# First layer of a spectral network: convolution and inverse column transform as one set of 32x32 matmuls

## Chip, cores and metric

The kernel runs on one core of one Trainium2 chip. The metric is the time of one execution on the device in microseconds; lower is better. All data are float32.

## What is computed

The input is a batch of 8 images, 8 channels, 256 x 256 pixels. Two residual steps follow each other. The first adds a small Fourier neural operator on the normalised input; the second adds a 3 x 3 dilation (a running maximum) of the normalised sum.

```python
x = x + fno(group_norm(x))
x = x + dilate3x3(group_norm(x))

def fno(x):                       # 4 groups of 2 channels; grid = row and column coordinate
    h = concat([x, grid])         # 4 inputs per group
    h = gconv1x1(h, fc0)          # 4 groups of 10 channels
    for i in range(4):
        h1 = spectral_conv(h)     # keep 24 x 12 frequencies, mix channels there, go back
        h2 = gconv1x1(h, w[i])
        h = h1 + h2
        if i < 3:
            h = gswish(h)
    return gconv1x1(gswish(gconv1x1(h, fc1)), fc2)   # 10 -> 128 -> 2 per group
```

fc0 is linear, so in the first layer it is folded into what follows: the first convolution h2 is a map from the two channels of x in a group (and constants) to ten channels, and its weights are the product of fc0 and w[0].

## The kernel before, in words

**State.** The state of a whole image stands in the tile `h`, 128 partitions x 11 chunks x 4 x 512. Image rows are spread over blocks, so that 32 partitions (a quarter, called q below) hold 3 blocks of 10 channels and two spare ones. Quarters are groups g in the layers with even number and parts of the rows in the odd ones; f counts the other of the two. One chunk c is 4 x 512 pixels for each partition.

**A layer.** `layers` runs four layers for each image. In each, `spectrum_h` (or `spectrum_x` ahead of layer 0) gets the small spectrum, `mix` multiplies it by the layer's weights and puts the result into the tile `fz`, and `rows_of` does the inverse transform along image rows with matmuls of `fz` against the table `rowg`, which leaves for each image row a vector of at most 32 spectral values in the tile `zt`: 24 of the transform, one constant, one linear term, six zeros. `layer` then goes over the 11 chunks. For each it issues a **burst** (line numbers of the profile in brackets):

- 16 matmuls of the 1x1 convolution, each on one 32x32 square of the array (L452; in layer 0 L449, where the moving operand is six rows of x and the weights are `wcn`)
- 8 matmuls of the inverse column transform, 256 columns each, `zt` as weights of 32 x 128 and the table `binv` as moving operand, added in PSUM (L455)
- two activations by ScalarE that empty the PSUM tiles `p_z` into `h` (L461, in layer 3 L463)

After the burst follow the transposes of the chunk before (`turn`, L424, copied by L194) and the forward transform of the chunk before that (`transform`, L437 and L438), and then steps of other work.

**x for layer 0.** The rows of x that layer 0 reads are loaded into `h` by `read_x` (L469): six partitions of each group and chunk, 4 loads of 48 KB a chunk, on SP's queue. A chunk of `h` is free for them when layer 3 of the image before has stored it in DRAM (L465).

**Other work beside it.** The output head of an image (fc1, fc2) runs beside the layers of the next image: `first` (L588, activation L590) and `second` (L610, added by VectorE at L615) work on slices of the stored state, loaded as `hs` on SP's queue (L580). The dilation of the image before that (`dilate`) runs in between on VectorE, with its loads on POOL's queue. The last head, that of image 7, runs alone.

**Order.** The program writes out the order of TensorE, VectorE and ScalarE by hand, through generators: each yields the number of head steps to be put at that place, for layers 0 to 2 by `CHUNK = (2, 1, 1)`, one entry per chunk in turn. The order on SP and POOL is chosen by the scheduler. PSUM is used as four tiles of two banks, handed out in turn:

```python
def ps_z(name):
    return ps.tile([128, 2, 512], F32, tag="z", bufs=4, name=name)
```

Each engine takes its instructions in order. The first layer of image 0 has no head beside it.

In `mix` for layer 0, L378 makes a constant from the mean, L379 adds it into `fz`, and L383 copies another row of constants; then `copy` (L194) brings the folded spectrum from PSUM into `fz`. The per-image scale (one over the standard deviation) is `mr[:, 1:2]`, and L476 multiplies the weights `wc` by it to give `wcn`.

Of the kernel before, what the change touches and what calls it, by code (L numbers as in the profile page):

```python
# [10 lines left out]
F32 = mybir.dt.float32  # L11
AF = mybir.ActivationFunctionType
ALU = mybir.AluOpType
# [5 lines left out]
HW = 256  # L19
NPIX = HW * HW  # L20
G = 4
WID = 10
# [10 lines left out]
NBLK = 3  # L33
NCH = 11
NQ = 4
# [10 lines left out]
def fno_dilate_kernel(ctx: ExitStack, tc: tile.TileContext, a: dict, out: bass.AP):  # L46
    nc = tc.nc
    mm = nc.tensor.matmul
    PE, DVE, ACT = mybir.EngineType.PE, mybir.EngineType.DVE, mybir.EngineType.Activation

    const = ctx.enter_context(tc.tile_pool(name="const", bufs=1))
    sb = ctx.enter_context(tc.tile_pool(name="sb", bufs=2))
# [10 lines left out]
    def part(i):  # L63
        return slice(32 * i, 32 * i + 32)
# [10 lines left out]
    def load(name, shape, eng=nc.gpsimd):  # L75
        t = const.tile(list(shape), F32, tag=f"c_{name}", name=f"c_{name}")
        eng.dma_start(t, a[name])
        return t

    load_x(0)  # L80
    beta_p = load("beta_p", (128, 4))
    beta_a = const.tile([128, 4 * G], F32, tag="c_beta_a", name="c_beta_a")
# [6 lines left out]
    fc0c = load("fc0c", (128, 3))  # L89
    wbd = load("wbd", (128, WID, G))  # L90
    wt = load("wt", (128, 4, G, 32))
    eh0 = load("eh0", (128, 3, 2, 32), nc.sync)
    xe = load("xe", (128, 6, G, 5), nc.sync)
    wext = const.tile([128, G, WID, 5], F32, tag="c_wext", name="c_wext")
# [3 lines left out]
    rowg = load("rowg", (128, NBLK, NQ, CS))  # L98
    binv = load("binv", (128, HW))
# [5 lines left out]
    edge = load("edge", (128, 4))  # L105

    h = const.tile([128, NCH, NQ, PIX], F32, tag="h", name="h")
    yin = const.tile([128, DR + 2, HW + 2], F32, tag="yin", name="yin")
    nc.vector.memset(yin, -BIG)
    y_rows = [dram.tile([C * HW + 2, HW], F32, tag=f"y{i}", bufs=1, name=f"y_rows{i}") for i in range(2)]  # L110
# [3 lines left out]
    zt = const.tile([128, CS, NQ, 32], F32, tag="zt", name="zt")  # L114
# [3 lines left out]

    def softplus(t, n, name):
        e = const.tile([128, n], F32, tag=f"{name}_e", name=f"{name}_e")
        nc.vector.tensor_scalar(e, t, -1.0, None, ALU.mult)
        nc.vector.tensor_tensor(e, e, t, ALU.max)
        nc.scalar.activation(e, e, AF.Exp, scale=-1.0)
        nc.vector.tensor_scalar(e, e, 1.0, None, ALU.add)
        nc.scalar.activation(e, e, AF.Ln)
        sp = const.tile([128, n], F32, tag=f"{name}_sp", name=f"{name}_sp")
        nc.vector.tensor_scalar(sp, t, 0.0, None, ALU.max)
        nc.vector.tensor_tensor(sp, sp, e, ALU.add)  # L130
        nc.vector.tensor_scalar(sp, sp, 1e-20, None, ALU.max)
        rs = const.tile([128, n], F32, tag=f"{name}_rs", name=f"{name}_rs")
        nc.vector.tensor_scalar(rs, sp, 1.1, None, ALU.mult)
        nc.vector.reciprocal(rs, rs)
        return sp, rs

    sp_p, rs_p = softplus(beta_p, 4, "bp")
    sp_a, rs_a = softplus(beta_a, 4 * G, "ba")  # L140
    io = const.tile([128, 4 * G], F32, tag="io", name="io")
    nc.vector.tensor_copy(io[:, 0:4], sp_a[:, 0:4])
    nc.vector.tensor_tensor(io[:, 4:12], sp_a[:, 4:12], rs_a[:, 0:8], ALU.mult)
# [3 lines left out]
        nc.vector.tensor_scalar(w2[:, g, :], w2[:, g, :], rs_a[:, 12 + g : 13 + g], None, ALU.mult)  # L147


    wc = const.tile([128, 32], F32, tag="wc", name="wc")  # L150
    p = ps_z("p_wc")
    for g in range(G):
        mm(p[32 * g : 32 * g + 6, 0, :32], fc0x[part(g), :], wt[part(g), 0, g, :], start=True, stop=True)
# [7 lines left out]
    nc.vector.memset(wm, 0.0)  # L161
    for g in range(G):
        nc.vector.tensor_scalar(wm[32 * g : 32 * g + 2, :, g], wc[32 * g : 32 * g + 2, :WID], -1.0, None, ALU.mult)
    cv = const.tile([3, WID, G], F32, tag="cv", name="cv")
    nc.vector.tensor_tensor(
        cv, p[:3, 1, : WID * G].rearrange("p (o g) -> p o g", o=WID),
        sp_a[:3, 0:4].unsqueeze(1).to_broadcast([3, WID, G]), ALU.mult,
# [177 lines left out]
    def mix(b, l, out_):  # L345

        s = [sb.tile([128, 3, G, 2, WID], F32, tag=f"S{i}", bufs=1, name=f"S{i}_{b}_{l}") for i in range(2)]
        bt, sw = out_["bt"], out_["sw"]
        for k in range(3):
            for k2 in range(2):  # L350
                pr = turned[:, 2, 1024 * k2 : 1024 * k2 + 800].rearrange("p (g m i) -> p g m i", g=G, i=WID)
                nc.vector.tensor_tensor(  # L352
                    pr, sw[k], bt[:, k2, k].unsqueeze(2).to_broadcast([128, G, 2 * WID, WID]), ALU.mult)
                yield 0.7
                nc.vector.tensor_reduce(  # L355
                    s[k2][:, k].rearrange("p g s o -> p (g s o)"),
                    pr.rearrange("p g m i -> p (g m) i"), AX.X, ALU.add,
                )
                if k == 0 and k2 == 1:
                    sw.append(load_sw(l, 2))  # L360
                yield 0.7
        f = sb.tile([128, 2, 3, G, WID], F32, tag="F", bufs=1, name=f"F_{b}_{l}")
        nc.vector.tensor_tensor(f[:, 0], s[0][:, :, :, 0, :], s[1][:, :, :, 1, :], ALU.subtract)
        nc.vector.tensor_tensor(f[:, 1], s[0][:, :, :, 1, :], s[1][:, :, :, 0, :], ALU.add)
        yield 0.5

        p = ps_a(f"p_f_{b}_{l}")
        for slot in range(2):
            for n, (table, part_of) in enumerate(((0, slot), (1 + slot, 1 - slot))):
                for q in range(4):  # L370
                    mm(p[part(q), 120 * slot : 120 * slot + 120], fold[part(q), table, :],
                       f[part(q), part_of].rearrange("p k g o -> p (k g o)"), start=n == 0, stop=n == 1)
        nc.vector.tensor_copy(fz[0:32, :, :, 24], cz[:, l])
        if l == 0:
            mr = out_["mr"]
            d = sb.tile([128, 1], F32, tag="d", name=f"dm_{b}")
            nc.vector.tensor_tensor(d, mr[:, 0:1], mr[:, 1:2], ALU.mult)
            mm(p[0:1, 240 : 240 + WID * G], d, wm.rearrange("p o g -> p (o g)"), start=True, stop=True)  # L378
            nc.vector.tensor_tensor(  # L379
                fz[0:1, :, :, 24], fz[0:1, :, :, 24],  # L380
                p[0:1, 240 : 240 + WID * G].rearrange("p (o g) -> p o g", o=WID), ALU.add)
        if l < 2:
            nc.vector.tensor_copy(fz[0:32, :, :, 25], cz[:, 4 if l == 0 else 3])  # L383
        for q in range(4):
            dst = fz[part(q), :, :, 6 * q : 6 * q + 6].rearrange("p o g k -> p k g o")
            src = p[part(q), :240].rearrange("p (k g o) -> p k g o", g=G, o=WID)
            copy(q, dst, src)
        yield 2.5
# [27 lines left out]
    def layer(b, l, out_, stored, side):  # L416
        group_in_f = l % 2 == 1
# [23 lines left out]

        def burst(c):
            pair = [ps_z(f"p_z_{b}_{l}_{c}_{i}") for i in range(2)]
            for f in range(NQ):
                for q in range(NQ):
                    o = pair[q // 2][part(f), q % 2, :]
                    if l == 0:
                        k = slice(32 * q, 32 * q + 6)
                        mm(o, wcn[k, :], h[k, c, f, :], start=True, stop=False)  # L449
                    else:  # L450
                        g = f if group_in_f else q
                        mm(o, wt[part(q), l, g, :], h[part(q), c, f, :], start=True, stop=False)  # L452
            for s in range(2):
                for q in range(NQ):
                    mm(pair[q // 2][:, q % 2, HW * s : HW * (s + 1)],  # L455
                       zt[part(q), 2 * c + s].rearrange("p f o -> p (f o)"), binv[part(q), :],
                       start=False, stop=s == 1)
            for i in range(2):
                dst = h[:, c, 2 * i : 2 * i + 2, :]
                if l < 3:  # L460
                    nc.scalar.activation(dst, pair[i], AF.Silu)  # L461
                else:
                    nc.scalar.activation(dst, pair[i], AF.Identity, bias=bias3)  # L463
            if l == 3:
                nc.sync.dma_start(stored[c], h[:, c].rearrange("p f w -> p (f w)"))  # L465

        def read_x(c):
            for g in range(G):
                nc.sync.dma_start(  # L469
                    h[32 * g : 32 * g + 6, c].rearrange("p f w -> p (f w)"), a["xp"][b, c, g])  # L470

        if l == 0:
            for c in range(NCH):
                read_x(c)
            wcn = sb.tile([128, 32], F32, tag="wcn", bufs=1, name=f"wcn_{b}")
            nc.vector.tensor_scalar(wcn, wc, out_["mr"][:, 1:2], None, ALU.mult)  # L476
        room = 0.0
        yield ()
        for c in range(NCH):
# [36 lines left out]
        yield from then  # L516


    spare = h.rearrange("p c f w -> p (c f w)")
    ya = spare[:, : 18 * (HW + 2)].rearrange("p (r w) -> p r w", r=18)  # L520
    ma = spare[:, 6144 : 6144 + 18 * HW].rearrange("p (r w) -> p r w", r=18)
    oa = spare[:, 12288 : 12288 + 16 * HW].rearrange("p (r w) -> p r w", r=16)
# [225 lines left out]
def _tables():  # L748
# [4 lines left out]
    real = row_of >= 0  # L753
# [20 lines left out]
    rowg[:, : NM + 1] = np.where(real, np.cos(ang), 0.0)  # L774
    rowg[:, NM + 1 : 2 * NM + 1] = np.where(real, np.sin(ang), 0.0)[1:]
    rowg[0, 2 * NM + 1] = np.where(real, line[row_of], 0.0)
    fold = np.zeros((4, 32, 3, 32))
    for i in range(2 * NM):
        m, sign = (i, 1.0) if i < NM else (2 * NM - i, -1.0)
# [9 lines left out]
    binv[:, at + 3] = -c * np.sin(_angle(np.outer(ky, w)))  # L789
    binv[:, 2 * NM] = 1.0  # L790
    binv[:, 2 * NM + 1] = line


    planes = [np.broadcast_to(line[:, None], (HW, HW)), np.broadcast_to(line, (HW, HW)), np.ones((HW, HW))]
    xe = np.zeros((4, 32, 2, 3, G, 5))
    for j, v in enumerate(planes):
# [12 lines left out]
        "rowg": rowg.reshape(128, NBLK, NQ, CS),  # L809
        "fold": fold.reshape(128, 3, 32), "binv": binv.reshape(128, HW),  # L810
        "xe": xe.reshape(128, 6, G, 5), "grp": grp, "edge": edge,
    }
    return {k: np.ascontiguousarray(v, f32) for k, v in tables.items()}

# [65 lines left out]
```

## Time and profile before

| | us |
|---|---|
| median of 3 runs | 4306.66 |
| lowest and highest run | 4306.16, 4310.51 |
| the profiled execution, its own time | 4309.43 |
| span of its instructions | 4307.7 |
| TensorE busy | 4089.1 |
| ScalarE busy | 2772.9 |
| VectorE busy | 2297.3 |
| layer-0 convolution matmuls (L449), busy | 115.0 |

The profile is of one execution. PE is TensorE's matmuls, PEld its weight loads, DVE VectorE, ACT ScalarE, SP the engine that issues most DMAs. A group of instructions is one row: line, engine, operation, output and inputs by the program's names, shapes, count, then the busy time in us and the mean duration in ns of one instruction, then the idle time of the engine just before them and what ended it. Each float32 matmul of the program appears as two instructions in the profile,[...] so the 1408 matmuls of L449 count 2816. Busy times of matmuls overlap, as up to 16 run together; what a group costs is seen from its start to the start of the next. In a timeline, the columns are the start and the length in us, the engine, the line, the operation and how many instructions were merged. In a row for a stretch, the columns are its ends, its length, the busy time (and number of instructions) of PE, PEld, DVE, ACT and POOL, then the granted clock of TensorE, the busy share of the DMA engines and GB/s.

### The profile page before, as it was taken

The page shows a single profiled execution, that of the slowest core. Times are in us where ns is not written, and L with a number is a line of the kernel's source. Part 1 is how long each engine was busy: PE and PEld are TensorE (multiplying, and loading weights), DVE is VectorE, ACT ScalarE, POOL GpSimd, SP SyncE. Part 2 cuts the span into 40 slices and gives each one's busy share as a digit, 9 for nine tenths or more (in the row PEclk, how much of TensorE's full clock was granted, in tenths as well). Part 3 has the DMA queues.
Part 4 walks back from the last instruction along what each step waited for, and adds up shares of the span by engine and source line. Part 5 has one row for each costly group of instructions (what it writes and reads, how often), then busy time and mean ns, then how long its engine had stood idle before and what let it go on. Part 6 is the DMA issues. An engine that isn't in the chain of part 4 may idle for free. (4 is left out here: it accounts for less than half of the span.)

```text
span 4307.7 us, 115455 instructions
## 1 busy us (share of the span) xinstructions
PE 4089.1 (95%) x52330; PEld 1925.6 (45%) x52330; DVE 2297.3 (53%) x3424; ACT 2772.9 (64%) x2886; POOL 117.0 (3%) x202
## 2 busy tenths in 40 slices
PE   5877999999999999999999999999999999999997
PEld 3544454444443444434444354444454444444222
DVE  4444544555655555655556555655655555654433
ACT  3435656766667666576666756667666766567887
POOL 1000000000000000000000000000000000000000
PEclk8988999999999999999999999999999999999999
DMA  2014101332114221242112511134111332114321
GB/s 78 13 40 151 53 28 43 135 103 62 55 53 161 87 62 52 75 171 58 52 59 81 182 42 53 50 104 159 55 45 53 136 120 62 48 57 147 109 60 46
DMA packets 113682, 344.65 MB, mean 80 GB/s; under 512 B 15611, under 2 KB 18107, under 8 KB 97768
## 3 DMA queue, kind: packets, MB, share of 16 engines
q1 hardware_dynamic: 95000, 276.18, 20.3%
q0 software_dynamic: 18192, 61.08, 4.3%
q8 instruction: 411, 6.73, 0.7%
q14 instruction: 79, 0.65, 0.1%
HBM read 213.21 MB, written 123.74 MB: 78 GB/s over the span
## 5 line engine op out<-in xcount | busy, mean ns | idle before, releaser
L590 ACT ACTIVATE act<-p_fc 128x1024 f32<-128x1024 f32 x2048 | 1968.9, 1025 | 1202.4 <-PE p_fc L588 1200.6
L588 PE MATMUL p_fc<-hs,c_w 32*128 32x512 f32 x8192 | 1191.6, 633 | 15.3 <-DVE turned L194 8.6
L610 PE MATMUL p_fc<-act,c_w 128*32 128x512 f32 x8192 | 986.7, 597 | 38.9 <-ACT act L590 25.6
L194 DVE COPY turned<-p_t 128x1024 f32<-128x1024 f32 x495 | 584.6, 1219 | 707.7 <-PE p_t L424 707.0
L588 PEld LDWEIGHTS p_fc<-hs,c_w 32*128 32x128 f32 x8192 | 383.6, 183 | 622.8 <-issue 240.9
L461 ACT ACTIVATE h<-p_z 128x1024 f32<-128x1024 f32 x528 | 512.9, 1023 | 117.4 <-PE p_z L455 116.7
L424 PE MATMUL p_t<-ident,h 128*128 128x128 f32 x4224 | 525.8, 278 | 0.0
L615 DVE TENSOR_TENSOR y<-p_fc,y 128x512 f32<-128x512 f32 x392 | 270.7, 690 | 474.9 <-PE p_fc L610 473.0
L610 PEld LDWEIGHTS p_fc<-act,c_w 128*32 128x32 f32 x8192 | 229.9, 109 | 647.4 <-issue 333.0
L424 PEld LDWEIGHTS p_t<-ident,h 128*128 128x128 f32 x4224 | 463.3, 142 | 98.5 <-ACT act L590 64.7
L455 PE MATMUL p_z<-c_binv,zt 32*128 32x256 f32 x5632 | 408.6, 404 | 1.0 <-ACT zt L192 1.0
L455 PEld LDWEIGHTS p_z<-c_binv,zt 32*128 32x128 f32 x5632 | 258.3, 185 | 304.4 <-issue 292.7
L452 PE MATMUL p_z<-h,c_wt 32*32 32x512 f32 x8448 | 317.0, 601 | 0.0
L437 PE MATMUL p_d<-turned,c_fw 128*32 128x240 f32 x4224 | 268.1, 371 | 4.1 <-ACT act L590 2.1
L194 DVE COPY zt<-p_g 128x264 f32<-128x264 f32 x300 | 159.0, 626 | 139.8 <-PE p_g L397 75.0
L463 ACT ACTIVATE h<-p_z,c_bias 128x1024 f32<-128x1024 f32 x176 | 186.6, 1111 | 26.4 <-PE p_z L455 25.9
L355 DVE TENSOR_REDUCE S<-turned 128x80 f32<-128x800 f32 x192 | 188.8, 983 | 5.0
L352 DVE TENSOR_TENSOR turned<-t,B 128x800 f32<-128x800 f32 x192 | 188.4, 981 | 0.5 <-DMA t<-in_spw 0.4
L452 PEld LDWEIGHTS p_z<-h,c_wt 32*32 32x32 f32 x8448 | 72.3, 103 | 190.1 <-ACT act L590 85.7
L437 PEld LDWEIGHTS p_d<-turned,c_fw 128*32 128x32 f32 x4224 | 109.6, 108 | 100.4 <-issue 39.1
L194 DVE COPY turned<-p_at 88x1024 f32<-88x1024 f32 x90 | 101.7, 1155 | 73.8 <-PE p_at L313 73.8
L438 DVE COPY zt<-p_d 128x240 f32<-128x240 f32 x264 | 105.5, 400 | 51.1 <-PE p_d L437 51.1
(170 smaller groups left out, 2023.8 us busy)
## 6 DMA issues: line engine op xcount, KB each, us to landing
stored<-h SPq DMA_DIRECT2D x88, 1024.0 KB
hs<-stored SPq DMA_DIRECT2D x352, 256.0 KB
t<-in_spw SPq DMA_DIRECT2D x96, 400.0 KB
yin<-y_rows POOLq DMA_DIRECT2D x56, 512.0 KB, 4.7
h<-in_xp SPq DMA_DIRECT2D x352, 48.0 KB
turned<-in_x SPq DMA_DIRECT2D x16, 1024.0 KB
y<-in_x SPq DMA_DIRECT2D x56, 256.0 KB
y_rows<-y POOLq DMA_DIRECT2D x56, 256.0 KB, 2.4
```

Of the source, the lines that this page charges most:

```text
L194: nc.vector.tensor_copy(dst, src)
L352: nc.vector.tensor_tensor(pr, sw[k], bt[:, k2, k].unsqueeze(2).to_broadcast([128, G, 2 * WID, WID]), ALU.mult)
L355: nc.vector.tensor_reduce(s[k2][:, k].rearrange("p g s o -> p (g s o)"), pr.rearrange("p g m i -> p (g m) i"), AX.X, ALU.add,)
L424: nc.tensor.transpose(t[:, i // 4, 128 * (i % 4) : 128 * (i % 4 + 1)], h[:, c, i // 2, 256 * (i % 2) + 128 * v : 256 * (i % 2) + 128 * (v ...
L437: mm(p[part(g), :240], fw[:, v, :], m[:, :, :, : NBLK * WID], start=v == 0, stop=v == 1)
L452: mm(o, wt[part(q), l, g, :], h[part(q), c, f, :], start=True, stop=False)
L455: mm(pair[q // 2][:, q % 2, HW * s : HW * (s + 1)], zt[part(q), 2 * c + s].rearrange("p f o -> p (f o)"), binv[part(q), :], start=False, s ...
L461: nc.scalar.activation(dst, pair[i], AF.Silu)
L588: mm(pair[g // 2][:, g % 2, :], w1[part(g), blk, :], hs[k][part(g), :], start=True, stop=True)
L590: nc.scalar.activation(act[:, 2 * i : 2 * i + 2, :], pair[i], AF.Silu)
L610: mm(acc[part(g), :], w2[:, g, 15 - rb - i : 47 - rb - i], act[:, g, :], start=i == 0, stop=i == 1)
L615: nc.vector.tensor_tensor(y, sums, y, ALU.add)
```

## The change

In layer 0 the two sets of matmuls of a burst become one. The six spare spectral values are used to carry the convolution: `mix` puts the convolution's weights, scaled by the image's `mr`, into columns 26 to 31 of `fz`, and the table `rowg` gets ones at these places, so that `rows_of` brings them into rows 26 to 31 of each 32 x 32 piece of `zt`. The moving operand has the matching rows in `h`: rows 0 to 25 of each group hold the first 26 rows of `binv`, repeated for each image row (the new table `wave`), and rows 26 to 31 hold the six rows of x. A matmul of a 32 x 32 piece of `zt` with 32 rows of `h` then gives the inverse transform and the convolution together. Each image row has its own piece, so a matmul covers 256 columns, and a burst has 32 of them.

`read_x` loads both parts for each chunk and image: 8 loads a chunk, four of 208 KB from `wave` and four of 48 KB from x. The product `wcn` of each image is replaced by `wsel`. Some small tiles of the setup are moved into the memory of `h` (chunk 10), which the first loads overwrite later.

```diff
+    xrow = load("xrow", (128, 38))
...
+    spare = h.rearrange("p c f w -> p (c f w)")
...
-    sp_p, rs_p = softplus(beta_p, 4, "bp")
-    sp_a, rs_a = softplus(beta_a, 4 * G, "ba")
+    sp_p, rs_p = softplus(beta_p, 4, 22300)
+    sp_a, rs_a = softplus(beta_a, 4 * G, 22320)
...
-    wc = const.tile([128, 32], F32, tag="wc", name="wc")
+    wc = spare[:, 22400:22432]
...
+    ws = spare[:, 22472:22482]
+    nc.vector.tensor_tensor(ws, wc[:, 0:WID], wc[:, WID : 2 * WID], ALU.add)
+    nc.vector.tensor_tensor(ws, ws, wc[:, 2 * WID : 3 * WID], ALU.add)
+    wk = const.tile([128, WID, 6], F32, tag="wk", name="wk")
+    nc.vector.tensor_tensor(
+        wk, ws.unsqueeze(2).to_broadcast([128, WID, 6]),
+        xrow[:, 0:6].unsqueeze(1).to_broadcast([128, WID, 6]), ALU.mult)
...
             nc.vector.tensor_tensor(
                 fz[0:1, :, :, 24], fz[0:1, :, :, 24],
                 p[0:1, 240 : 240 + WID * G].rearrange("p (o g) -> p o g", o=WID), ALU.add)
+
+            wsel = sb.tile([128, 32], F32, tag="wsel", bufs=1, name=f"wsel_{b}")
+            nc.vector.tensor_scalar(wsel, xrow[:, 6:38], mr[:, 1:2], None, ALU.mult)
+            pair = [ps_z(f"p_wk_{b}_{i}") for i in range(2)]
+            for g in range(G):
+                mm(pair[g // 2][0:32, g % 2, : 6 * WID], wsel[part(g), :],
+                   wk[part(g)].rearrange("p o i -> p (o i)"), start=True, stop=True)
+            for i in range(2):
+                nc.vector.tensor_copy(
+                    fz[0:32, :, 2 * i : 2 * i + 2, 26:32].rearrange("p o g i -> p g o i"),
+                    pair[i][0:32, :, : 6 * WID].rearrange("p g (o i) -> p g o i", o=WID))
...
-            for f in range(NQ):
-                for q in range(NQ):
-                    o = pair[q // 2][part(f), q % 2, :]
-                    if l == 0:
-                        k = slice(32 * q, 32 * q + 6)
-                        mm(o, wcn[k, :], h[k, c, f, :], start=True, stop=False)
...
+            if l == 0:
+
+                for s in range(2):
+                    cols = slice(HW * s, HW * (s + 1))
+                    for f in range(NQ):
+                        for q in range(NQ):
+                            mm(pair[q // 2][part(f), q % 2, cols], zt[part(q), 2 * c + s, f, :],
+                               h[part(q), c, f, cols], start=True, stop=True)
...
                 nc.sync.dma_start(
-                    h[32 * g : 32 * g + 6, c].rearrange("p f w -> p (f w)"), a["xp"][b, c, g])
+                    h[32 * g : 32 * g + 26, c].rearrange("p f w -> p (f w)"), a["wave"])
+                nc.sync.dma_start(
+                    h[32 * g + 26 : 32 * g + 32, c].rearrange("p f w -> p (f w)"), a["xp"][b, c, g])
...
-            wcn = sb.tile([128, 32], F32, tag="wcn", bufs=1, name=f"wcn_{b}")
-            nc.vector.tensor_scalar(wcn, wc, out_["mr"][:, 1:2], None, ALU.mult)
...
+    for blk in range(NBLK):
+        rowg[0, 26 + blk, blk] = real[blk]
...
+    xrow = np.zeros((4, 32, 38))
+    for i in range(6):
+        xrow[:, i, i] = 1.0
+        xrow[:, i, 6 + 26 + i // 2] = 1.0
...
+        "xrow": xrow.reshape(128, 38), "wave": np.tile(binv[0, :26], (1, 2 * NQ)),
```

More of the change, by code (lines that the diff above doesn't have):

```diff
@@ L117, in fno_dilate_kernel, with softplus @@
     nc.vector.memset(fz, 0.0)
-    def softplus(t, n, name):
-        e = const.tile([128, n], F32, tag=f"{name}_e", name=f"{name}_e")
+    def softplus(t, n, at):
+        e = spare[:, at + 0 * n : at + 1 * n]
         nc.vector.tensor_scalar(e, t, -1.0, None, ALU.mult)
@@ L127, in softplus @@
         nc.scalar.activation(e, e, AF.Ln)
-        sp = const.tile([128, n], F32, tag=f"{name}_sp", name=f"{name}_sp")
+        sp = spare[:, at + 1 * n : at + 2 * n]
         nc.vector.tensor_scalar(sp, t, 0.0, None, ALU.max)
@@ L131, in softplus @@
         nc.vector.tensor_scalar(sp, sp, 1e-20, None, ALU.max)
-        rs = const.tile([128, n], F32, tag=f"{name}_rs", name=f"{name}_rs")
+        rs = spare[:, at + 2 * n : at + 3 * n]
         nc.vector.tensor_scalar(rs, sp, 1.1, None, ALU.mult)
@@ L163, in fno_dilate_kernel @@
         nc.vector.tensor_scalar(wm[32 * g : 32 * g + 2, :, g], wc[32 * g : 32 * g + 2, :WID], -1.0, None, ALU.mult)
-    cv = const.tile([3, WID, G], F32, tag="cv", name="cv")
+    cv = spare[:3, 22432:22472].rearrange("p (o g) -> p o g", o=WID)
+    ws = spare[:, 22472:22482]
[5 more added lines that the diff above has]
+        xrow[:, 0:6].unsqueeze(1).to_broadcast([128, WID, 6]), ALU.mult)
     nc.vector.tensor_tensor(
@@ L443, in burst @@
             pair = [ps_z(f"p_z_{b}_{l}_{c}_{i}") for i in range(2)]
-            for f in range(NQ):
-                for q in range(NQ):
-                    o = pair[q // 2][part(f), q % 2, :]
-                    if l == 0:
-                        k = slice(32 * q, 32 * q + 6)
[L449 to L457, printed above, removed]
+            if l == 0:
[5 more added lines that the diff above has]
+                               h[part(q), c, f, cols], start=True, stop=True)
+            else:
+                for f in range(NQ):
+                    for q in range(NQ):
+                        mm(pair[q // 2][part(f), q % 2, :], wt[part(q), l, f if group_in_f else q, :],
+                           h[part(q), c, f, :], start=True, stop=False)
+                for s in range(2):
+                    for q in range(NQ):
+                        mm(pair[q // 2][:, q % 2, HW * s : HW * (s + 1)],
+                           zt[part(q), 2 * c + s].rearrange("p f o -> p (f o)"), binv[part(q), :],
+                           start=False, stop=s == 1)
             for i in range(2):
@@ L516, in layers @@
         yield from then
-    spare = h.rearrange("p c f w -> p (c f w)")
     ya = spare[:, : 18 * (HW + 2)].rearrange("p (r w) -> p r w", r=18)
```

## The prediction

> **What bounds the kernel now.** I read the busy shares first, then the chain of waits, then the groups by line, then stretches of the timeline.
>
> ```profile
> PE 4089.1 (95%) x52330; PEld 1925.6 (45%) x52330; DVE 2297.3 (53%) x3424; ACT 2772.9 (64%) x2886; POOL 117.0 (3%) x202
> L455 PE MATMUL p_z<-c_binv,zt 32*128 32x256 f32 x5632 | 408.6, 404 | 1.0 <-ACT zt L192 1.0
> L452 PE MATMUL p_z<-h,c_wt 32*32 32x512 f32 x8448 | 317.0, 601 | 0.0
> L449 PE MATMUL p_z<-h,wcn 6*32 6x512 f32 x2816 | 115.0, 600 | 2.4 <-issue 1.4 <-ACT zt L192 0.8 <-DVE turned L194 0.2
> ```
>
> TensorE is busy 95% of the span, and an idle time of 2.4 us in front of all 88 bursts of L449 says that it does not wait there. The page's chain of waits covers only the last stretch, the head of image 7 running alone, so it says nothing of layer 0; the stretches do. In a table of the eight layer-0 stretches, this is the one of image 2:
>
> ```profile
> 916.00:1003.00 87.00, 85.90 (x1096) 43.64 (x1068) 43.70 (x61) 54.45 (x57) 2.07 (x4) 0.98 0.10 30
> ```
>
> PE 85.9 of 87 us, VectorE 43.7, ScalarE 54.5. A busy TensorE need not be doing useful work, so I took costs from start to start, in one chunk of that stretch (timeline, ScalarE's lines with it):
>
> ```profile
> 947.51 1.14 PE L588 MATMUL p_fc<-hs,c_w 32*128 32x512 f32 x8
> 948.59 1.18 PE L449 MATMUL p_z<-h,wcn 6*32 6x512 f32 x32
> 948.75 1.94 ACT L590 ACTIVATE act<-p_fc 128x1024 f32<-128x1024 f32 x2 [0.99 <-PE p_fc L588]
> 949.70 1.15 PE L455 MATMUL p_z<-c_binv,zt 32*128 32x256 f32 x16
> 950.77 1.97 PE L424 MATMUL p_t<-ident,h 128*128 128x128 f32 x16
> 950.88 1.94 ACT L461 ACTIVATE h<-p_z 128x1024 f32<-128x1024 f32 x2 [0.19 <-PE p_z L455]
> 952.67 1.02 PE L437 MATMUL p_d<-turned,c_fw 128*32 128x240 f32 x16
> 953.62 1.14 PE L588 MATMUL p_fc<-hs,c_w 32*128 32x512 f32 x8
> ```
>
> Each group begins as the one before ends: the burst takes 948.59 to 950.77, that is 1.11 us for the convolution and 1.07 for the inverse transform, 2.18 together. The unit that counts in layer 0 is TensorE time per burst.
>
> [...] the 32 instructions of one L449 group (each matmul is two passes) last 600 ns each, and start to start the group takes 1.11 us. [...]
>
> ```profile
> 48.91 21.94 SPq L469 DMA_DIRECT2D h<-in_xp  x36
> 378.92 21.98 SPq L469 DMA_DIRECT2D h<-in_xp  x30
> ```
>
> give 0.61 and 0.73 us per issue.
>
> **The change, part by part.** *The burst.* Out go 16 matmuls of 512 columns over 16 squares and 8 of 256 columns over four row strips. In come 32 of 256 columns, two for each square, so four passes of 256 columns through a square where L449 has two of 512: the same 1024 columns. Two rows bound the price from below: L449 itself (1.11) and L455, four passes of 256 on four strips (1.07). From above: a matmul lasts 600 ns at 512 columns and 404 at 256, so about 0.21 us is fixed; if the array empties between the halves, 1.11 + 0.21 = 1.32. No group of before sends four passes through all 16 squares, so I take the middle, 1.2. A burst then saves 2.18 - 1.2 = 0.98 us, and 8 images x 11 chunks = 88 bursts save 86 us.
>
> *What becomes late.* The burst was cover for ScalarE. In the chunk above, both PSUM tiles of the head step at 947.51 are emptied by ScalarE from 948.75 to 950.69, 0.97 us each. The transposes that follow the burst reuse them: now at 950.77, after both; then at 949.79, when the first is just free, and its half of L424 (0.95) lasts until the second is. The next steps meet the burst's own tiles (emptied by ScalarE, which goes straight on, at 951.66 and 952.63) at 951.69 and 952.64. So nothing stalls yet, but no margin is left. I charge 0.1 us for each of the 77 chunks with a head beside them: +8 (0 to 0.5 each).
>
> *In mix, once an image.* wcn becomes wsel (0.21 us on VectorE either way), but it stands behind the addition L379, which waits for L378, and the eight new matmul instructions wait for wsel. TensorE, in order, stands for two VectorE operations (about 0.5 us with the signals), then runs 60 columns twice (about 0.4, from L371's 285 ns each): 0.9 x 8 = +7. Behind it wait the next head steps. The two copies into fz (nearest row: 583 ns for 240 elements, so 0.4 each) delay the fz copies; for images 2 to 7 two head steps stand between and hide it (the fz copies end at 900.57, their reader L397 starts at 901.84, and it moves back too), for images 0 and 1 it is exposed: +2.
>
> *Setup.* One more load on POOL's queue (0.56 us of issue ahead of cz, fold and others) and three small VectorE operations: +1. The scratch tiles moved into h are free long before chunk 10 is loaded.
>
> *The loads.* 352 transfers become 704, all on SP, with 73 MB more (352 x 208 KB), against 276 MB on that queue now. [...] the hardware queue's row (276.18 MB in 20.3% of 16 engines' span) makes 0.41 us of 8 KB on average[...] I take 5. What must not be late:
>
> - Image 0: 36 of its 44 loads go out only from 48.91 on. Chunk 10 then lands near 49 + 2 + 50 = 101, and is read at 70 + 10 x 3.9 = 109. Hidden at 5[...].
> - Later images: loads follow the stores of layer 3 (one every 8.2 us, 863.43 to 896.28). Store, head load and the new loads make 3.3 + 0.5 + 5 = 8.8 per chunk on the engines; the excess of 0.6 x 11 = 7 us falls on what stands behind in SP's order, the head's loads of hs and the y loads. A load of hs issued at 882.32 is used at 908.79, 26 us later. Hidden.
> - Image 1: layer 3 of image 0 runs without a head, so 30 loads stood in a row until 400.9, and hs loads behind them; now 20 to 25 us later. I charge 4 in all for images 0 and 1.
>
> Sum: -86 + 8 + 7 + 2 + 1 + 4 = -64 us on the profiled execution, 4309.4 (span 4307.7), so 4245; the median of the runs lies 2.8 below that execution, so **4242 us**.
>
> **The rivals.** *The loads become the bound (slower).* [...] It beats the gain from roughly 7.4 us a chunk. [...] *The squares queue for weights (slower).* If the second half's weights load one square after another, 16 x 0.103 us (L449's load) make a burst of 2.75: 88 x 1.55 more, 4380. L455 and L402 reload in every pass without it, though on four places only. *The time turns into waits for PSUM.* If ScalarE's emptying sets the chunk, only the 11 chunks of image 0 keep the gain: 11 gained less 14 of the other costs, 4310. ScalarE's 54 of 87 us speaks against it. *Part of the gain is lost to late loads in images 0 and 1*, 20 to 40 us: about 4270. That the burst does not shrink at all would need the 16 squares to fail, which L449 excludes.
>
> **How the numbers follow.** Forecast 0.61 (alone 4215 to 4268: burst 1.1 to 1.32, tile waits 0 to 0.3); late loads in part 0.13; PSUM waits 0.05; loads as the bound 0.15; queued weights 0.06. About 0.2% (9 us) is what a measurement here can tell from no change. Faster is the first two less a little, 0.73; the same 0.05; slower 0.22. The range runs from the forecast's lower end to a load pace just past the crossing: 4213 to 4340; beyond it lies most of the two slow cases.
>
> **What would show it.** One group in place of L449 and L455 in layer 0, with 1.1 to 1.3 us from its start to that of L424; 88 bursts, 5632 instructions of 256 columns. Image 0's chunk period 3.9 instead of 4.9 us; layer-0 stretches near 77 instead of 87. SP's issues of L469 at about 0.6 us. Wrong if TensorE shows idle time ended by the loads of h or of hs, if the group takes over 1.4 us, or if L424 waits for ScalarE by more than 0.3 us a chunk.

## The result, and the profile after

The changed kernel takes **4378.35 us** (median of 4 runs, 4375.64 to 4388.06) against 4307.84 (4306.16 to 4310.51) for the kernel before: a ratio of 1.0167, 95% interval 1.015 to 1.0185. The forecast was 4242 and faster; the kernel is 70 us slower. The profiled execution took 4375.64 us, its span 4373.7, that is 66.0 more than the span before.

Line numbers have moved. L471 is the new burst (before L449 and L455), L445 the transposes after it (L424), L458 the transform (L437), L480 and L476 the inverse transform and the convolution of layers 1 to 3 (L455, L452). L612 and L634 are the head's two layers (L588, L610), L637 its first addition into y (L613), L604 and L627 the loads of hs and y (L580, L603), L490 the store (L465), L494 and L496 the loads of wave rows and of x.

From the page of the kernel after, the busy shares, the groups of instructions and the loads:

```profile
PE 4044.6 (92%) x53802; PEld 1925.0 (44%) x53802; DVE 2302.0 (53%) x3443; ACT 2766.3 (63%) x2886; POOL 117.7 (3%) x203
...
L480 PE MATMUL p_z<-c_binv,zt 32*128 32x256 f32 x4224 | 303.4, 400 | 0.6 <-ACT zt L202 0.6
L471 PE MATMUL p_z<-h,zt 32*32 32x256 f32 x5632 | 145.1, 403 | 10.4 <-ACT act L614 7.2
L637 DVE SCALAR_TENSOR_TENSOR y<-p_fc,c_b,y 128x512 f32<-128x512 f32 x56 | 42.1, 751 | 217.2 <-DMA y<-in_x 159.0
...
h<-in_wave SPq DMA_DIRECT2D x352, 208.0 KB
h<-in_xp SPq DMA_DIRECT2D x352, 48.0 KB
```

The change is there: 5632 matmuls in layer 0 in place of 2816 + 1408, and the inverse transform is left to layers 1 to 3. TensorE's busy time fell by 45 us while the span rose by 66, so idle time has come in. The row that names its cause is none of the changed lines: L637, VectorE's addition of the head's sums to y, stood idle for 217.2 us, 159.0 of them until a load of y landed. The stretch of image 2's layer 0, the one shown of before:

```profile
916.00:1003.00 87.00, 73.50 (x1148) 40.35 (x1144) 39.65 (x54) 47.48 (x51) 1.30 (x2) 0.86 0.28 77
```

TensorE is busy for 73.5 of 87 us instead of 85.9, at a granted clock of 0.86 instead of 0.98, with a DMA share of 0.28 instead of 0.10. The waits (in total, times, longest) of the kernel after, from TensorE's, VectorE's and SP's tables:

```profile
PE p_fc L612 <- DVE mr_y L214: 55.0, 4, 17.5
...
PE p_fc L612 <- DVE y L637: 29.5, 2, 16.6
...
DVE y L637 <- DMA y<-in_x: 159.0, 6, 29.2
...
SPq L494 <- DMA h<-in_wave: 127.7, 176, 4.2
```

Six waits of VectorE for y, and six stops of TensorE behind VectorE (the first two rows, 55.0 + 29.5 = 84.5 us together): one for each of images 2 to 7. There was no such row before. In the last row SP itself waits, in the row of new loads, until earlier loads of the row have landed.

**One stop from its cause to its end**, in image 2. SP's timeline, the last store of layer 3 and then the last of the new loads with what stood behind them:

```profile
889.59 0.35 SPq L490 DMA_DIRECT2D stored<-h  x1
...
928.79 0.31 SPq L494 DMA_DIRECT2D h<-in_wave  x1
929.18 0.27 SPq L496 DMA_DIRECT2D h<-in_xp  x1
930.29 0.35 SPq L604 DMA_DIRECT2D hs<-stored  x1
930.74 0.38 SPq L627 DMA_DIRECT2D y<-in_x  x1
```

Of the image's 88 loads, 47 are issued after that store, and they fill 40 us (with other loads between them); before, 5 of 44 were. Only when the last is out does SP come to y, at 930.74. In the kernel before:

```profile
912.26 0.33 SPq L603 DMA_DIRECT2D y<-in_x  x1
```

So y is issued 18.5 us later, though TensorE had reached the step earlier than before, and VectorE can go on 5.4 us after that, at 936.15. VectorE's timeline of the kernel after:

```profile
936.15 0.75 DVE L637 SCALAR_TENSOR_TENSOR y<-p_fc,c_b,y 128x512 f32<-128x512 f32 x1 [24.47 <-DMA y<-in_x]
936.82 0.15 DVE L214 COPY mr_y<-p_st_y 128x1 f32<-128x1 f32 x1
937.33 2.35 DVE L204 COPY turned<-p_t 128x1024 f32<-128x1024 f32 x2
```

VectorE takes these instructions in the written order: it stands before the addition for 24.47 us, and behind it wait the statistics (L214, at 936.82) and the copies out of the transposes (L204, at 937.33), which TensorE needs. TensorE's timeline:

```profile
922.39 3.68 PE L445 MATMUL p_t<-ident,h 128*128 128x128 f32 x16 [1.05 <-ACT h L486]
936.96 2.14 PE L612 MATMUL p_fc<-hs,c_w 32*128 32x512 f32 x8 [10.89 <-DVE mr_y L214]
...
939.74 2.83 PE L471 MATMUL p_z<-h,zt 32*32 32x256 f32 x64
...
1481.47 1.14 PE L612 MATMUL p_fc<-hs,c_w 32*128 32x512 f32 x8
1482.54 1.50 PE L471 MATMUL p_z<-h,zt 32*32 32x256 f32 x64
1483.96 1.97 PE L445 MATMUL p_t<-ident,h 128*128 128x128 f32 x16
```

TensorE issues what it can and stands for 10.89 us. The last three lines are an undisturbed chunk: there the burst takes 1.42 us from its start to that of L445, and L612 and L471 last half as long as just after the stop.

**The ledger.** I took TensorE's time from the start of each group to the start of the next (the group's slot), summed by line, and compared the two executions. The burst gives 57.7 back (its own waits in it). The transposes, in whose slots the stops fall, take 89 more; the head's first layer 9.6, mix 8, the statistics 8, the transform 5 and the spectral rows 3. The sum is +65, of the 66 in the spans.

### The profile page after: what moved, and what is told of

The parts are those of the page before. It is cut to its first block, busy times and chain, and to the rows that moved or that the text cites. A ratio compares the mean times of both kernels' runs of the same rounds, so it can differ in the third digit from the quotient of the medians.

```text
span 4373.7 us, 118951 instructions
## 1 busy us (share of the span) xinstructions
PE 4044.6 (92%) x53802; PEld 1925.0 (44%) x53802; DVE 2302.0 (53%) x3443; ACT 2766.3 (63%) x2886; POOL 117.7 (3%) x203
## 5 line engine op out<-in xcount | busy, mean ns | idle before, releaser
L612 PE MATMUL p_fc<-hs,c_w 32*128 32x512 f32 x8192 | 1203.0, 637 | 105.8 <-DVE mr_y L214 55.0
L634 PE MATMUL p_fc<-act,c_w 128*32 128x512 f32 x8192 | 987.4, 597 | 38.0 <-ACT act L614 25.5
L204 DVE COPY turned<-p_t 128x1024 f32<-128x1024 f32 x495 | 584.7, 1220 | 637.9 <-PE p_t L445 637.2
L612 PEld LDWEIGHTS p_fc<-hs,c_w 32*128 32x128 f32 x8192 | 387.1, 184 | 718.1 <-issue 226.7
L445 PE MATMUL p_t<-ident,h 128*128 128x128 f32 x4224 | 530.4, 280 | 6.8 <-ACT h L486 6.4
L445 PEld LDWEIGHTS p_t<-ident,h 128*128 128x128 f32 x4224 | 467.1, 143 | 113.8 <-ACT act L614 70.6
L634 PEld LDWEIGHTS p_fc<-act,c_w 128*32 128x32 f32 x8192 | 230.5, 109 | 646.0 <-issue 338.2
L476 PE MATMUL p_z<-h,c_wt 32*32 32x512 f32 x8448 | 318.0, 601 | 0.3 <-issue 0.3
L480 PE MATMUL p_z<-c_binv,zt 32*128 32x256 f32 x4224 | 303.4, 400 | 0.6 <-ACT zt L202 0.6
L480 PEld LDWEIGHTS p_z<-c_binv,zt 32*128 32x128 f32 x4224 | 192.7, 184 | 227.7 <-issue 220.5
L458 PE MATMUL p_d<-turned,c_fw 128*32 128x240 f32 x4224 | 268.1, 371 | 3.1 <-ACT act L614 2.1
L204 DVE COPY zt<-p_g 128x264 f32<-128x264 f32 x300 | 160.3, 624 | 140.0 <-PE p_g L418 74.2
L476 PEld LDWEIGHTS p_z<-h,c_wt 32*32 32x32 f32 x8448 | 72.3, 103 | 191.3 <-ACT act L614 87.2
L637 DVE SCALAR_TENSOR_TENSOR y<-p_fc,c_b,y 128x512 f32<-128x512 f32 x56 | 42.1, 751 | 217.2 <-DMA y<-in_x 159.0
L471 PE MATMUL p_z<-h,zt 32*32 32x256 f32 x5632 | 145.1, 403 | 10.4 <-ACT act L614 7.2
L458 PEld LDWEIGHTS p_d<-turned,c_fw 128*32 128x32 f32 x4224 | 109.7, 108 | 99.4 <-issue 38.7
```

What stands on the lines that cost most here:

```text
L204: nc.vector.tensor_copy(dst, src)
L445: nc.tensor.transpose(t[:, i // 4, 128 * (i % 4) : 128 * (i % 4 + 1)], h[:, c, i // 2, 256 * (i % 2) + 128 * v : 256 * (i % 2) + 128 * (v ...
L458: mm(p[part(g), :240], fw[:, v, :], m[:, :, :, : NBLK * WID], start=v == 0, stop=v == 1)
L476: mm(pair[q // 2][part(f), q % 2, :], wt[part(q), l, f if group_in_f else q, :], h[part(q), c, f, :], start=True, stop=False)
L480: mm(pair[q // 2][:, q % 2, HW * s : HW * (s + 1)], zt[part(q), 2 * c + s].rearrange("p f o -> p (f o)"), binv[part(q), :], start=False, s ...
L612: mm(pair[g // 2][:, g % 2, :], w1[part(g), blk, :], hs[k][part(g), :], start=True, stop=True)
```

## The experiments

The theory, called Q in the expectations: what costs is the order of SP's queue, in which the load of y stands behind the wave rows' loads. The rival, called B: the 73 MB and the transfers themselves cost, wherever they stand. Each ratio is against the kernel before, run on the same chip.

**Move only the load of y to POOL's queue (y_on_pool).** Edit of the kernel after:

```diff
                 box["y"] = y
-                nc.sync.dma_start(
+                nc.gpsimd.dma_start(
                     y, a["x"][b].rearrange(...)[:, t])
```

> The changed kernel with the y loads issued on POOL's queue in place of SP's. Theory Q (the y load of a new head stands behind the loads of wave and x in SP's order, VectorE waits for it, the transposes' copies and with them TensorE wait for VectorE): the 159 us that VectorE waits for y go below 30, the 15 to 20 us stops of TensorE in chunk 1 of images 2 to 7 go, about 4275 to 4300. Rival B (73 MB more traffic slows all transfers): y is late on the other queue too, 4360 to 4380. Rival P (the loss lies on TensorE's own work): no change, 4370 to 4380.

4272.42 us (4271.48 to 4273.27), ratio 0.992 (0.9904 to 0.9937). One word takes 106 us off the changed kernel, with all 704 loads still on SP, and makes it faster than before. That is a little better than Q's 4275. VectorE's wait for y is gone. B can't explain that, for not a byte less is moved, and P can't either, for TensorE's own work is the same. In the stretch of image 2's layer 0 the DMA engines are busier than in the changed kernel (0.39 against 0.28), and TensorE loses nothing:

```profile
916.00:1003.00 87.00, 85.71 (x1352) 44.45 (x1356) 48.57 (x69) 58.52 (x62) 4.99 (x8) 1.00 0.39 104
```

At most the 24 us by which this run lies above the run without these loads (no_wave_loads, below) are left for B. A part of them is a late load of hs in image 1:

```profile
435.99 2.09 PE L612 MATMUL p_fc<-hs,c_w 32*128 32x512 f32 x8 [6.93 <-DMA hs<-stored]
```

The rest of the 24 us was not followed.

**The wave rows' loads alone, in the kernel before (wave_loads_alone).** The rows are loaded and read by no one:

```diff
+                nc.sync.dma_start(
+                    h[32 * g + 6 : 32 * g + 32, c].rearrange("p f w -> p (f w)"), a["wave"])
                 nc.sync.dma_start(
                     h[32 * g : 32 * g + 6, c].rearrange("p f w -> p (f w)"), a["xp"][b, c, g])
```

> The kernel before with the 352 loads of wave added, into 26 rows of h that its layer 0 does not read; its matmuls are untouched. Q: the same order on SP and the same late y load, so slower than before by what the stops cost, 80 to 110 us: 4390 to 4415. B: the same, 4380 to 4415. P: the loads cost nothing, 4308.

4414.59 us (4410.28 to 4418.14), ratio 1.0251 (1.0236 to 1.0266). VectorE's waits:

```profile
DVE y L615 <- DMA y<-in_x: 146.9, 6, 25.9
```

The same six waits come up with the old burst. The loss belongs to the loads, not to the matmuls: 108 us of it without any of the rest of the change. This rules out P; Q and B expected nearly the same here.

**The change without these loads (no_wave_loads).** Only image 0 gets them:

```diff
-                nc.sync.dma_start(
-                    h[32 * g : 32 * g + 26, c]..., a["wave"])
+                if b == 0:
+                    nc.sync.dma_start(
+                        h[32 * g : 32 * g + 26, c]..., a["wave"])
```

> The changed kernel with the loads of wave left out for images 1 to 7 (those images' layer 0 then multiplies what layer 3 left in these rows). Q and B: the price of the loads goes and the burst's saving stays (88 x 0.75 = 66, less 8 in mix): 4255 to 4275. P: 4370 to 4380.

4247.93 us (4247.05 to 4253.02), ratio 0.9867 (0.9852 to 0.9881), a little under what was expected. This is the price of everything in the change but 308 loads: 58 us less than before. The loads of images 1 to 7 cost 4378 - 4248 = 130 us. The stretch:

```profile
916.00:1003.00 87.00, 85.88 (x1310) 45.89 (x1314) 51.59 (x70) 56.11 (x59) 3.13 (x5) 1.00 0.15 44
```

In this stretch TensorE is as busy as before the change, at full clock.

**One load for a chunk instead of eight, still on SP (one_load).** The host's table holds wave rows and x together, so 1 MB goes in one transfer:

```diff
-            for g in range(G):
-                nc.sync.dma_start(h[32 * g : 32 * g + 26, c]..., a["wave"])
-                nc.sync.dma_start(h[32 * g + 26 : 32 * g + 32, c]..., a["xp"][b, c, g])
+            nc.sync.dma_start(h[:, c].rearrange("p f w -> p (f w)"), a["xw"][b, c])
```

> The changed kernel with one load of 1 MB per chunk, wave and x laid out together in DRAM by the host, in place of eight: the same bytes into the same rows, 88 transfers in place of 704. Q: SP is free 30 us earlier, y is not late: 4250 to 4275, faster than both. B: the bytes are the same, so 4350 to 4380. P: 4370 to 4380.

4338.06 us (4335.71 to 4342.22), ratio 1.0075 (1.006 to 1.009). My number was missed: y is now on time, but another load is late. VectorE's wait and SP's wait:

```profile
DVE turned L362 <- DMA t<-in_spw: 82.9, 8, 29.9
...
SPq L493 <- DMA stored<-h: 589.7, 74, 10.1
```

and SP's wait in the kernel before:

```profile
SPq L469 <- DMA stored<-h: 292.8, 67, 6.2
```

SP's timeline with the single load:

```profile
907.86 0.33 SPq L493 DMA_DIRECT2D h<-in_xw  x1
908.28 0.45 SPq L352 DMA_DIRECT2D t<-in_spw  x1
...
917.36 0.33 SPq L493 DMA_DIRECT2D h<-in_xw  x1
917.78 0.38 SPq L352 DMA_DIRECT2D t<-in_spw  x1
...
927.22 0.33 SPq L493 DMA_DIRECT2D h<-in_xw  x1
```

In the program a chunk's load comes after the store that empties its rows. SP stands at that wait until the store has landed, 74 times, for 589.7 us, and each of mix's loads of spectral weights (L352) leaves only after it, 9 to 10 us apart. It is the same fault with another victim: a load that waits, ahead of one that is needed. Whether SP's waits or the bytes are the cause is what the next run asks.

**The same single load on POOL's queue (one_load_on_pool).**

```diff
-            nc.sync.dma_start(h[:, c]..., a["xw"][b, c])
+            nc.gpsimd.dma_start(h[:, c]..., a["xw"][b, c])
```

> The one-load kernel with its loads of 1 MB issued on POOL's queue in place of SP's. Its run showed TensorE stopped where mix waits for its third weight load (83 us of VectorE), which stands behind an x load that waits for a store to land. Theory Q (whatever stands behind the x loads in SP's order is late, not the bytes): SP never waits for a store any more, weights, hs and y are on time, 4245 to 4265. Rival B (bytes): 4325 to 4345 as before. A third outcome: y_rows and yin on POOL become the late ones, 4290 to 4340.

4260.46 us (4257.33 to 4261.85), ratio 0.9891 (0.9874 to 0.9907): faster than both kernels, by 48 us than before and by 118 than the change as it stood. It moves the same bytes. SP's timeline and the stretch:

```profile
911.83 0.33 SPq L623 DMA_DIRECT2D y<-in_x  x1
```

```profile
916.00:1003.00 87.00, 85.87 (x1333) 44.66 (x1302) 48.65 (x67) 58.54 (x62) 3.13 (x5) 1.00 0.16 46
```

y goes out at 911.83, about when it did before (912.26), and the stretch is that of no_wave_loads. This kernel is 12 us slower than that one. In image 1, mix (L381) waits 20.3 us where it waits 9.3 there, but TensorE comes to it earlier, so the two profiled executions are only 4.3 us apart; the 12 us were not followed further.

**All eight loads a chunk on POOL (eight_loads_on_pool)** asks whether the queue alone is enough. In the kernel after, both lines of the load become `nc.gpsimd.dma_start`.

> The changed kernel with all eight loads a chunk on POOL's queue in place of SP's. Q (only the order on SP mattered): near the one-load kernel on POOL, 4260 to 4275. Rival C (their count costs on any queue, POOL's own y_rows and yin then stand behind them): 4290 to 4350.

4308.73 us (4305.36 to 4312.48), ratio 1.0005 (0.9996 to 1.0014): no change against before. Q's number was missed; the count costs too. The stretch, in which the last of the five engines is POOL:

```profile
916.00:1003.00 87.00, 83.81 (x1212) 43.57 (x1204) 43.85 (x63) 54.24 (x58) 16.39 (x31) 0.96 0.34 84
```

POOL spends 16.39 us here where a single load a chunk needed 3.13, and the DMA share is 0.34 instead of 0.16. Against one_load_on_pool 48 us are lost, in the head's first layer (18), the burst (11), the inverse transform and mix of image 1. I did not find one place or one mechanism for it: it stays open how much is POOL's issue and how much the small transfers.

**Relief of SP alone, in the kernel before (x_on_pool_before)**: its 352 loads of x become `nc.gpsimd.dma_start`. This asks whether POOL's version is faster only because SP had been too full all along.

> The kernel before with its 352 loads of x on POOL's queue and nothing else. Q: before loses nothing to the order on SP (y is on time by 8 us), so 4300 to 4312, and what the changed kernel gains with its loads on POOL is the burst's. Rival (a relieved SP speeds up any version): under 4290.

4312.16 us (4308.16 to 4317.22), ratio 1.0014 (1.0007 to 1.0021). Nothing is gained, so the 48 us of one_load_on_pool are put down to the burst. The test is not quite clean: it issues 352 small loads on POOL, and as eight_loads_on_pool, with 704, is 48 us above one_load_on_pool, with 88, a small gain from a relieved SP could be hidden.

**Why the burst takes 1.42 us and not 1.2.** In the trace of the undisturbed chunk, the first half's squares start about 7 ns apart, and their second passes follow from 240 ns on. The 33rd matmul instruction, by its place the first of the second half, starts at 456 ns, 216 ns after the second pass before it, so without a stop. The 34th starts only at 649 ns, 193 ns later, and the others follow 17 ns apart instead of 7. Three other orders, each in the kernel y_on_pool with nothing else changed:

```diff
# order_s_q_f
-                    for f in range(NQ):
-                        for q in range(NQ):
+                    for q in range(NQ):
+                        for f in range(NQ):
# order_pairs
-                for s in range(2):
-                    for f in range(NQ):
+                for p, s in ((0, 0), (0, 1), (1, 0), (1, 1)):
+                    for f in (2 * p, 2 * p + 1):
# order_f_s_q
-                for s in range(2):
-                    for f in range(NQ):
+                for f, s in ((f, s) for f in range(NQ) for s in range(2)):
+                    for _ in range(1):
```

> The same with order s, q, f: the four squares of one row strip follow each other. W: the first half's start is slower, the group 1.4 to 1.8. D: 1.43 as before.

> The same with the strips in pairs, s inside: 8 squares, their second halves, then the other 8. W: a square comes again after 8; 1.1 to 1.3 if the pairs overlap, about 1.7 to 2.0 if not. D: 1.9 to 2.1.

> The kernel with y on POOL, burst order strip f outermost, then half s, then q: a square's second half follows after 4 matmuls. The group takes 1.43 us with s outermost. Theory W (the second half's weights are admitted in program order, so that a square that comes again late, after the whole first half, waits): coming again after 4 gives no stop between halves but four strips in a row; 1.1 to 1.2 if the strips overlap, 2 to 3.5 if only four squares run at a time. Rival D (all 16 squares must drain before any second half begins): the strips drain four times, over 2.5.

One run each: 4267.76, 4290.95 and 4324.31 us. TensorE's timeline of the three, the burst and what follows it:

```profile
1452.88 1.49 PE L471 MATMUL p_z<-h,zt 32*32 32x256 f32 x64
1454.30 0.88 PE L445 MATMUL p_t<-ident,h 128*128 128x128 f32 x6
```

```profile
1466.53 1.79 PE L471 MATMUL p_z<-h,zt 32*32 32x256 f32 x64
1468.26 0.98 PE L445 MATMUL p_t<-ident,h 128*128 128x128 f32 x7
```

```profile
1465.35 2.22 PE L471 MATMUL p_z<-h,zt 32*32 32x256 f32 x64
1467.51 0.66 PE L445 MATMUL p_t<-ident,h 128*128 128x128 f32 x4
```

In the chunks shown, all 16 squares before a return (twice through them in all) costs 1.42 us, in either order of row and column (as a median of all bursts 1.43 and 1.48); a return after 8 squares costs 1.73, after 4 squares 2.16. The sooner the order turns back to squares just used, the longer the group, with the same 32 matmuls in it. D, that all 16 squares must drain first, is out: it asked for 1.9 to 2.1 after 8 squares and for over 2.5 after 4. W's ranges hold, but for the two last orders only those that it gave for squares that do not overlap well; that the order of the weights is the reason is not shown. The times follow roughly: 88 x (1.73 - 1.42) = 27 and 88 x (2.16 - 1.42) = 65 over y_on_pool's 4272 would be 4299 and 4337, against 4291 and 4324.

**Is it the 256 columns, or the return? (conv_twice)** The kernel before, with layer 0's convolution of 512 columns issued twice into the same place; the second result overwrites the first:

```diff
-            for f in range(NQ):
+            for rep_, f in ((r, f) for r in range(2 if l == 0 else 1) for f in range(NQ)):
...
-                        mm(o, wcn[k, :], h[k, c, f, :], start=True, stop=False)
+                        mm(o, wcn[k, :], h[k, c, f, :], start=True, stop=rep_ == 0)
```

> The kernel before with layer 0's sixteen convolution matmuls of 512 columns issued twice in a row with the same result (the first set is overwritten): each square is visited a second time, as in the change, but after a pass of 512 columns. The group of one set takes 1.11 us from start to start. Theory V (each return of a square to a second matmul, sixteen matmuls later, costs about 0.3 us whatever its length): 1.11 + 0.85 + 0.3 = 2.3 us. Rival L (only the short 256-column passes leave too little time to load weights): 1.11 + 0.85 = 1.96 us. Whole kernel: V 4306 + 88 x 1.2 = 4412, L 4383.

One run, 4438.78 us. TensorE's timeline:

```profile
1043.97 2.35 PE L449 MATMUL p_z<-h,wcn 6*32 6x512 f32 x64
1046.24 1.13 PE L455 MATMUL p_z<-c_binv,zt 32*128 32x256 f32 x13
```

The doubled group takes 2.27 us where the single one took 1.11. That is some 0.3 more than was expected without a price for the return (1.96), and what was expected with it (2.3). So the return costs about 0.3 us here whether the pass before has 256 columns (1.42 us in the changed kernel, against the 1.11 of L449) or 512. The trace has the same form as well: the first return starts at 882 ns, 429 ns after the pass before it and so without a stop, the next at 1076, 194 ns later, and the others follow 17 ns apart. Why the array stops there is not shown. The whole run is 26 us above the figure expected with it: L449 gives 107 of the 132 us, the transposes 15, the inverse transform 8; the rest was not followed.

## Why the prediction was wrong

**The failed step** is the second of the loads: "the excess of 0.6 x 11 = 7 us falls on what stands behind in SP's order, the head's loads of hs and the y loads. A load of hs issued at 882.32 is used at 908.79, 26 us later. Hidden." Three things in it were wrong. First, the slack of one load was given to all. The next y load of the kernel before was issued at 912.26, and VectorE used it at 920.95:

```profile
920.95 0.75 DVE L613 SCALAR_TENSOR_TENSOR y<-p_fc,c_b,y 128x512 f32<-128x512 f32 x1 [5.27 <-PE p_fc L610]
```

It had 8.7 us, not 26. Second, the delay is not 7 us but 18.5: I spread the loads evenly behind the stores, chunk by chunk, where SP's fixed order puts 47 of the 88 behind the last store. Third, the step did not ask what stands behind the reader of y. VectorE, in its written order, holds the copies of the transposes behind that addition, so a late y stops the layer and not only the head. The cost charged was nothing for the later images and 4 us for images 0 and 1; the loads cost 130 us, of which 106 go when the y load alone is moved.

**The pace of the loads was nearly right.** "I take 5" was an estimate, which no row of the kernel before shows; the 8.8 us a chunk and the excess of 0.6 were built on it. SP's timeline in a row of loads of image 1 reads

```profile
386.40 0.31 SPq L494 DMA_DIRECT2D h<-in_wave  x1
...
387.69 0.31 SPq L494 DMA_DIRECT2D h<-in_wave  x1
...
389.13 0.31 SPq L494 DMA_DIRECT2D h<-in_wave  x1
```

about 1.35 us for a pair, 5.4 for a chunk. In image 2 the 47 loads behind the last store take 40 us, which is 6.7 for a chunk. Image 0 was hidden, as the step said; its bursts follow each other every 4.3 us, where 3.9 was foretold, and every 5.0 before, not 4.9. In image 1 TensorE stops 5.0 us for a load of hs, about the 4 charged.

**The burst was mis-sized.** "I take the middle, 1.2" was 1.42 in the chunk shown and 1.43 as a median, above the range of 1.11 to 1.32. The upper bound charged 0.21 us for the array running empty, a matmul's fixed time as estimated from the 600 ns at 512 columns and the 404 at 256; the return costs 0.3, the stop of 0.19 and the wider spacing of the later squares together. The saving is 88 x (2.18 - 1.43) = 66 us, not 86.

**PSUM waits: none.** "+8" was charged for the transposes behind ScalarE; in no_wave_loads the transposes' slots add up to 504.5 us against 509.5 before. Whether a burst of 1.2 us would have brought these waits no run shows.

**Mix was right in the main.** 7 was foretold, and the slots of its small matmuls grew from 7.0 to 15.1 us, +8. The 2 for images 0 and 1 was not found as a cost of its own.

With these terms, -66 + 0 + 8 is -58 without the wave loads, which is what no_wave_loads shows. That its 4248 comes near the forecast of 4242 is in part luck: 20 us too much for the burst, against some 15 us of charges that did not come. The rest of the difference is the loads.

**The rivals.** "The loads become the bound" had the side right, but by the wrong measure. It asked from which pace of the loads the gain is lost (7.4 us a chunk). The pace stayed at 5.4 to 6.7, and y was late all the same. "The squares queue for weights" has the size of its burst wrong, 1.42 instead of 2.75, though the second half does start more slowly. "Part of the gain is lost to late loads in images 0 and 1" came true for 5.0 us. Of my own signs for a wrong prediction, the third (a wait of the transposes for ScalarE) appeared only in the six disturbed chunks, about 1 us each, the second (over 1.4 us) just appeared, and the first, idle time ended by h or hs, appeared only in these 5.0 us: the tile to look at was y.

## What to carry to other kernels

Before putting loads on a queue, list everything behind them with its own slack, from issue to use, and take the smallest: here y had 8.7 us, and behind the new loads on SP it was issued 18.5 us later. In one_load the loads that waited for a store held what followed them on SP, 74 times, for 589.7 us; so such a load belongs on a queue where nothing urgent stands behind it, in as few transfers as possible: with the same bytes on POOL's queue, one load a chunk took 4260 us and eight took 4309. Then ask of the late load's reader what its engine holds in order behind it, as VectorE, standing for 24.47 us before the addition to y, held the copies of the transposes. And price a packed group of matmuls by how soon it comes back to the same squares, not by columns alone: the same 32 matmuls took 1.42 us with a return after 16 squares, 1.73 after 8 and 2.16 after 4.

## What the runs showed of the hardware that was not expected

In these bursts a return to the same squares cost about 0.3 us after sixteen of them (conv_twice: 2.27 us, where 1.96 was expected without a price), and more the sooner it came: 1.42, 1.73 and 2.16 us for the same 32 matmuls after 16, 8 and 4 squares. Not every return had this price. In the kernel before, the instructions of one group of L455 (at 949.70, two passes of each of two matmuls on four row strips) start in fours at 0, 320, 536 and 752 ns. From the second four on they are 216 ns apart, and within a four about 7 ns: the return with new weights at 536 brings no stop.

Around a stop of TensorE the work itself slows: just after the 10.89 us that end at 936.96, L612 lasts 2.14 us instead of 1.14 and L471 2.83 instead of 1.50. But the granted clock had fallen before the stop began, at 926.07. Three stretches of the kernel after, then two of the kernel before:

```profile
917.40:920.80 3.40, 2.25 (x70) 1.22 (x66) 0.00 (x0) 1.94 (x2) 0.00 (x0) 1.00 0.83 180
922.30:926.10 3.80, 3.68 (x16) 3.28 (x16) 0.00 (x0) 0.95 (x2) 0.00 (x0) 0.50 0.72 196
937.00:944.60 7.60, 7.48 (x84) 4.57 (x85) 2.87 (x6) 5.39 (x6) 0.00 (x0) 0.50 0.23 76
...
920.50:924.00 3.50, 3.50 (x46) 0.98 (x42) 1.29 (x4) 3.09 (x4) 0.00 (x0) 1.00 0.00 0
924.00:927.40 3.40, 3.40 (x35) 2.30 (x22) 0.00 (x0) 0.97 (x2) 0.00 (x0) 0.50 0.00 0
```

The transposes at 922.39 already take 3.68 us, against 1.97 in the undisturbed chunk. The clock is back at 1.00 from 945 on, some 8 us after the stop has ended. In the kernel before it falls to half for 3.4 us at the same place. No long idle time of TensorE stands ahead of either fall: in the 15 us before it the longest gap is 0.25 us in the kernel before and 0.86 us in the changed kernel. What brings it down is not shown. In images 2 to 7 the changed kernel runs at half clock for 126 us in layer 0, with TensorE busy for 56 of them. At full clock that work would take about 28 us less, half of the 56, as an estimate from the durations above (1.14 us for 2.14, 1.50 for 2.83), beside the 84.5 us of the stops. With y alone moved (y_on_pool), the stretch 916 to 1003 runs at a clock of 1.00, so this too is counted as a part of what a late y costs.
